# A hand-ordered graph network kernel: spreading a few groups' target columns on TensorE, and a new order for the first turn, the last groups and the value products

## Chip, cores and metric

The kernel runs on one NeuronCore of one Trainium2 chip. The metric is the device time in microseconds of one execution. The core has TensorE (matmuls; its weight loads are shown apart), VectorE, ScalarE, GpSimd (called POOL in the profile) and SyncE, whose queue (SP) issues the transfers.

## What is computed

The input x is 128 graphs of 128 nodes with 256 features, in float32, and adj an integer adjacency matrix of 128 x 128 for each graph (values 0 and 1). Two layers follow each other, each with an attention over the graph, a feed-forward part of 256 to 1024 to 256 and two layer norms:

```python
# layer 0
q, k = x @ Wq + bq, x @ Wk + bk                      # 8 heads of 32
attn = softmax(q k^T / sqrt(32))
out  = sum over r of (attn * (adj == r)) @ (x @ Wv[r] + bv[r])
x = norm(x + out @ Wo + bo)
x = norm(x + gelu(x @ W1 + b1) @ W2 + b2)
# layer 1: two graph attentions, one after the other
def gat(h, W, a):
    Wh = h @ W
    e = leaky_relu(Wh @ a[:F] + transpose(Wh @ a[F:]), 0.2)   # source + target
    return softmax(where(adj > 0, e, -9e15), axis=1) @ Wh
h = norm(x + gat(gat(x, V1, a1), V2, a2))
out = norm(h + relu(h @ U1 + c1) @ U2 + c2)
```

The target term is one number for each node, and it has to be added along the other axis of the 128 x 128 edge matrix: a column of 128 partitions must become a row that all 128 partitions hold. This is the "spread" that the change touches.

## The kernel before, in words

**Groups.** The 128 graphs are cut into 32 groups of G = 4 (512 tokens; NG = 32). All work of a group is on tiles of 128 partitions. A second, general pass stands behind a flag that a few checks compute at the end (`checks`, L755; `pflag`, L858); with these inputs it doesn't run.

**Steps.** Each stage of a group is a Python generator that issues its instructions up to a `yield`; one such piece is a step below. `in_order(...)` (L530) takes generators with counts, and functions, and calls them in turn. So the order in which each engine receives its instructions is written out by hand; nothing is rearranged later. The engines run at their own pace and wait for each other by semaphores.

The generators and their steps:

- `projections` (L552), 8 steps: four products for q and k (tile pq, L560; biased by ScalarE, L564), then four value products, one for each graph (tile pv, L570; VectorE adds the bias into v, L574). They are called pv0 to pv3 in this document.
- `attention` (L647): scores (tile ps, L588; exp on ScalarE into e, L594), mask (pm, L602), sums (denominator pden, L615; pav, L624; two reciprocals, L639 and L641), for two pairs of graphs, then the output product (pwo, L662), which `added` adds to x with the statistics of the norm (L310 to L317).
- `norm` (L358), 4 steps. The first is `root`: VectorE adds epsilon to the variance (rs, L324), GpSimd raises it to the power -1/2 (L325). The second is `normed`: for norms 0 to 2, VectorE forms the shift sh (L333) and ScalarE applies scale and shift to the four blocks of x (L338); for norm 3, VectorE does it (L343). The third and fourth are `scaled`: VectorE multiplies x by a row and adds a row (L356).
- `turned(S, i)` (L370): eight transposes of x into two PSUM tiles (pt, L290), scaled out to yT by ScalarE (L293), and, where a feed-forward follows, four combinations of quarters of yT on VectorE (yS, L378 to L381). i says after which norm. "Turn (31,2)" below is `turned` of group 31 after norm 2.
- `ffn` (L383), 22 steps: both products in a seven-product form (Strassen-Winograd), whose forms are B11, T3, T2, B21, T1, T4 and B22. Steps 1 to 6 and 8 are B11, T3, T2, B21, T1, T4, B22 for the first half of the hidden units; step 7 is B11 for the second half, steps 9 to 14 the rest of it (L400). Steps 15 to 21 are the seven products of the second matrix (L409), 22 the statistics of pair 0. Some products accumulate on a PSUM bank that ScalarE has copied from another (`seeded`, L438, L472, L487); two others are copied out as p7 and p16 (tile p, L445 and L449), and T1 of each half may only start on the bank once p16 is copied. After each, ScalarE applies the activation (L424) and VectorE adds (L455, L459, L468 to L470; L492 to L513 in the second product).
- `layer1` (L705), 12 steps: the product with the combined weights (pw, L713; two steps), the spread of the targets (step 3), the edge weights in three steps (gs: ScalarE adds source and target, L686; leaky ReLU on VectorE, L690, and exp on ScalarE, L691; mask and normalising on VectorE, L695 to L702), the product py (L726, step 7), the second spread (step 8), three steps of edge weights again, and the product pg (L738) with `added` for norm 2 (step 12).

`spread` (L669) turns the four columns of a group into one 4 x 128 line by one transpose (L672), copies the line to SBUF (L674), sends it to HBM and back as a broadcast to 128 partitions (two transfers on SP's queue, L677 and L678).

**The turns.** The main loop (`for g in range(NG - 1)`, L794) interleaves three groups. Its turn g runs the first feed-forward of group g+1 (f1) and the second of group g (f2), the attention of group g+2 (pr for projections, at for attention), the layer norms n0 to n3, layer 1 of group g in the first half and the first part of layer 1 of group g+1 in the second half. `g == 0` has an order of its own. The turn with g = 30 has no group g+2 (`more` is false). Behind the loop the last group's norm, layer 1 and second feed-forward are written out, then the checks and the last norm, which is done in pairs of graphs so that a pair can be stored while the other is still computed.

The explicit `exp` and `gelu` entries (L526) load ScalarE's function table ahead of its use.

PSUM: four banks rotate under the tag "s" (pq, pv, ps, pden, pt, pw, py, pg, pr); four single banks are for the feed-forward products (three) and pav.

Of the kernel before, what the change touches and what calls it, by code (L numbers as in the profile page):

```python
# [106 lines left out]
def fast_pass(ctx, tc, a, out):  # L107
# [47 lines left out]
    def entered(g):  # L155

        xt = load_xT(g)
        ad, xr = load_rest(g)
        return dict(xt=xt, ad=ad, x=xr, g=g)
# [3 lines left out]
    first = dict(g=0, xt=load_xT(0))  # L163
# [134 lines left out]
    def pair(p):  # L298
        return slice(2 * p, 2 * p + 2)
# [27 lines left out]
    def normed(S, i, bs=slice(0, G)):  # L327
# [3 lines left out]
        if i < 3:  # L331
            sh = small.tile([P, G], F32, tag="sh", name=f"sh_{i}_{S['g']}")
            nc.vector.scalar_tensor_tensor(  # L333
                sh, mv[:, :, 0], -1.0, rs, op0=ALU.mult, op1=ALU.mult
            )
        for b in range(bs.start, bs.stop):
            if i < 3:
# [331 lines left out]
    def spread(columns, n):  # L669

        pr = ps_s.tile([P, T], F32, tag="s", name="pr_" + n)
        nc.tensor.transpose(pr[:G, :P], columns, k.ident)  # L672
# [32 lines left out]
    def layer1(S):  # L705
# [14 lines left out]
        target = spread(wh[:, :, D + 3], n + "_0")  # L720
# [10 lines left out]
        target = spread(yh[:, :, D + 1], n + "_1")  # L731
# [42 lines left out]
    with tc.manual_schedule(engines={ET.PE, ET.Activation, ET.DVE, ET.SP, ET.Pool}):  # L774
# [19 lines left out]
        for g in range(NG - 1):  # L794
# [8 lines left out]
            ready = (lambda: prepared(S2)) if more else (lambda: None)  # L803
            if g == 0:
                in_order((f1, 2), n1_, pr, (f1, 2), lambda: turned(S, 1), (n1_, 2))
                l1 = layer1(S)
                in_order(
                    f1, l1, f1, l1, f1, l1, (f1, 2), pr, (f1, 4), pr, f1, (l1, 3), f1, pr, f1, l1, f1,
                    l1, pr, f1, pr, f1, (l1, 3), f1, pr, f1, l1, n2, (at, 2), f1, n2, f1, n1, pr,
                    lambda: turned(S, 2), (at, 3),  # L810
                )
            else:
                n3 = norm(st[g - 1], 3)
                in_order(
                    pr, lambda: turned(S1, 0), pr, f1, f2_, n3, f1, n0_, (f1, 4), n0_, (f1, 2), n3, l1, f1, f1, l1, n3,
                    (f1, 3), pr, n3, lambda: store(st[g - 1]), f1, f1, exp, l1, l1, pr, f1, l1, f1,
                    f1, l1, n2, f1, at, n2, at, f1, pr, lambda: turned(S, 2), pr, (at, 3), f1, f1, pr, n1,
                )
            if not more:
# [3 lines left out]
                f2, pr, f2, n1, (n2, 2), f2, at, (f2, 2), lambda: turned(S1, 1), (f2, 2), at, (n1, 2),  # L823
                (f2, 2), l1, at, ready, (f2, 4), l1, f2, at, f2, l1, (f2, 2), at, at, f2, at, n0, l1, f2,
                n0, l1, gelu, f2, l1, f2,
            )
            n0_, f2_ = n0, f2
        in_order((f2, 2), n1, (f2, 2), lambda: turned(S1, 1), (n2, 2))
        l1 = layer1(S1)
        in_order(  # L830
            f2, (l1, 2), f2, l1, (n1, 2), (f2, 8), (l1, 3), f2, l1, f2, l1, (f2, 4), (l1, 3), f2, l1,
        )
        n2, n3 = norm(S1, 2), norm(S, 3)
        in_order(n2, f2, n2, (f2, 2), lambda: turned(S1, 2))
# [4 lines left out]
        for p in (1, 0):  # L839
# [5 lines left out]
            if p == 1:  # L845
                in_order((f2, 2))
# [345 lines left out]
```

## Time and profile before

| | |
|---|---|
| device time, 3 runs | 2836.33 us median (2835.97 to 2838.88) |
| span of the profiled execution | 2837.9 us |
| mean granted TensorE clock | 0.991 |
| TensorE busy, 0 to 71 us / 71 to 142 / 142 to 213 | 59.3 / 66.3 / 67.4 of 71 us |
| TensorE busy, 300 to 1200 us | 898.6 of 900 us |
| TensorE busy, 2694 to 2765 / 2765 to 2838 us | 60.2 of 71 / 46.5 of 73 us |
| granted clock there | 0.91 / 0.83 |
| VectorE, ScalarE busy, whole span | 2176.8, 1568.5 us |
| transfers of the spread back from HBM | 64 of 256 KB, 4.2 us to landing |

A page of this profile shows each engine's busy time, its share of the span and its instructions; then the span in 40 slices, in tenths. A line of the waits says which engine's instruction waited for which other, for how long in total, how often, and the longest. In a timeline, a line is a start in us, a duration, engine, source line, operation, what is written and read, and a count of equal instructions merged; brackets hold the idle time before and what ended it. The duration of a merged matmul line reaches to the modelled end of the last one, so the distance between two starts says more of the pace than the duration does. A float32 matmul shows as two instructions: `x4` is two matmuls.

### The profile page before, as it was taken

The page shows a single profiled execution, that of the slowest core. Times are in us where ns is not written, and L with a number is a line of the kernel's source. Part 1 is how long each engine was busy: PE and PEld are TensorE (multiplying, and loading weights), DVE is VectorE, ACT ScalarE, POOL GpSimd, SP SyncE. Part 2 cuts the span into 40 slices and gives each one's busy share as a digit, 9 for nine tenths or more (in the row PEclk, how much of TensorE's full clock was granted, in tenths as well). Part 3 has the DMA queues.
Part 4 walks back from the last instruction along what each step waited for, and adds up shares of the span by engine and source line. Part 5 has one row for each costly group of instructions (what it writes and reads, how often), then busy time and mean ns, then how long its engine had stood idle before and what let it go on. Part 6 is the DMA issues. An engine that isn't in the chain of part 4 may idle for free.

```text
span 2837.9 us, 51798 instructions
## 1 busy us (share of the span) xinstructions
PE 2776.8 (98%) x20816; PEld 2233.8 (79%) x20816; DVE 2176.8 (77%) x5068; ACT 1568.5 (55%) x3395; POOL 162.2 (6%) x153
## 2 busy tenths in 40 slices
PE   8999999999999999999999999999999999999986
PEld 4778788887888887888887887887887887888875
DVE  6677887877787877777877777778778778878765
ACT  3545555556555556555556565556556555555552
POOL 3000000000000000000000000000000000000000
PEclk9999999999999999999999999999999999999998
DMA  6010110010111010111010111000110001110000
GB/s 173 5 27 15 32 35 34 24 34 12 34 35 34 23 35 12 35 34 34 23 35 12 35 34 34 24 26 21 34 35 27 31 15 32 35 34 23 16 16 20
DMA packets 70645, 87.27 MB, mean 31 GB/s; under 512 B 8192, under 2 KB 48512, under 8 KB 70400
## 3 DMA queue, kind: packets, MB, share of 16 engines
q1 hardware_dynamic: 69568, 83.52, 9.5%
q8 instruction: 164, 2.69, 0.4%
q14 instruction: 81, 0.66, 0.1%
q10 hardware_dynamic: 832, 0.40, 0.0%
HBM read 66.99 MB, written 16.91 MB: 30 GB/s over the span
## 4 chain that ended last, share of the span: by engine, by line
PE 86%; ACT 7%; DVE 2%; issue 0%; POOL 0%; POOLq 0%; DVEq 0%; ACTq 0%
PE ph L400 14%; PE po L409 14%; PE seeded L409 12%; PE seeded L400 11%; PE pq L560 7%; PE pv L570 6%; PE pw L713 4%; PE pav L624 4%; ACT x L338 4%; PE pwo L662 4%; PE pt L290 3%; PE pden L615 2%; PE py L726 2%; PE pg L738 2%; ACT e L594 1%; PE ps L588 1%
## 5 line engine op out<-in xcount | busy, mean ns | idle before, releaser
L338 ACT ACTIVATE x<-x,sh,rs 128x256 f32<-128x256 f32 x384 | 199.4, 597 | 180.5 <-DVE sh L333 180.5
L325 POOL TENSOR_TENSOR rs<-rs,mhalf 128x4 f32<-128x4 f32 x129 | 138.8, 1076 | 2635.0 <-DVE rs L324 2225.5
L594 ACT ACTIVATE e<-ps 128x512 f32<-128x512 f32 x256 | 131.8, 601 | 209.1 <-PE ps L588 209.1
L570 PE MATMUL pv<-wv,xT 128*128 128x512 f32 x512 | 242.3, 597 | 0.3 <-ACT e L594 0.3
L400 PE MATMUL seeded<-yS,w_L_gnn_w_ff 128*128 128x256 f32 x768 | 207.3, 392 | 5.0 <-ACT seeded L472 1.3
L400 PE MATMUL seeded<-yS,w_L_gnn_W 128*128 128x256 f32 x768 | 204.0, 388 | 2.4 <-ACT seeded L472 1.3
L455 DVE TENSOR_TENSOR hT<-seeded,p 128x512 f32<-128x512 f32 x128 | 88.5, 692 | 148.3 <-PE seeded L400 148.3
L400 PE MATMUL ph<-yT,w_L_gnn_w_ff 128*128 128x256 f32 x768 | 199.0, 388 | 0.0
L310 DVE BATCH_NORM_STATS2 st<-x 128x6 f32<-128x256 f32 x512 | 192.5, 418 | 7.7
L400 PE MATMUL ph<-yT,w_L_gnn_W 128*128 128x256 f32 x768 | 194.4, 382 | 2.4 <-ACT yT L293 2.4
L409 PE MATMUL po<-w_L_gnn_W,hT 128*128 128x128 f32 x1536 | 190.1, 277 | 0.0
L409 PE MATMUL po<-w_L_gnn_w_ff,hT 128*128 128x128 f32 x1536 | 187.0, 275 | 0.0
L409 PEld LDWEIGHTS po<-w_L_gnn_w_ff,hT 128*128 128x128 f32 x1536 | 184.0, 192 | 3.2
L409 PEld LDWEIGHTS po<-w_L_gnn_W,hT 128*128 128x128 f32 x1536 | 181.7, 192 | 5.7 <-issue 0.5
L400 PEld LDWEIGHTS seeded<-yS,w_L_gnn_W 128*128 128x128 f32 x768 | 138.4, 190 | 52.7 <-issue 15.6
L400 PEld LDWEIGHTS seeded<-yS,w_L_gnn_w_ff 128*128 128x128 f32 x768 | 137.8, 190 | 48.9 <-ACT p L449 24.6
L400 PEld LDWEIGHTS ph<-yT,w_L_gnn_W 128*128 128x128 f32 x768 | 144.2, 191 | 38.0 <-ACT yT L293 10.2
L400 PEld LDWEIGHTS ph<-yT,w_L_gnn_w_ff 128*128 128x128 f32 x768 | 139.2, 191 | 38.3 <-issue 13.9
L602 DVE TENSOR_TENSOR pm<-e,adj 128x512 f32<-128x512 f32 x256 | 161.7, 693 | 4.1 <-ACT e L594 4.1
L686 ACT ACTIVATE gs<-spread,wh 128x128 f32<-128x128 f32 x128 | 40.9, 390 | 187.1 <-DMA spread<-hbm 187.1
L424 ACT ACTIVATE hT<-hT,c_L_gnn_b 128x256 f32<-128x256 f32 x256 | 109.4, 497 | 61.4 <-DVE hT L455 60.3
L570 PEld LDWEIGHTS pv<-wv,xT 128*128 128x128 f32 x512 | 90.7, 192 | 66.1 <-issue 63.6
(155 smaller groups left out, 6116.4 us busy)
## 6 DMA issues: line engine op xcount, KB each, us to landing
xT<-in_xT_dram SPq DMA_DIRECT2D x32, 512.0 KB, 7.1
x<-in_x_dram SPq DMA_DIRECT2D x32, 512.0 KB, 8.3
spread<-hbm SPq DMA_DIRECT2D x64, 256.0 KB, 4.2
out_dram<-x SPq DMA_DIRECT2D x31, 512.0 KB, 2.9
adj<-in_adjT_dram SPq DMA_DIRECT2D x32, 256.0 KB, 6.0
w_L_gnn_W<-in_L_gnn_W_dram SPq DMA_DIRECT2D x8, 256.0 KB, 7.3
w_L_gnn_w_ff<-in_L_gnn_w_ff_dram SPq DMA_DIRECT2D x8, 256.0 KB, 5.1
hbm<-line SPq DMA_DIRECT2D x64, 2.0 KB
```

Source lines behind the costliest of these rows:

```text
L310: nc.vector.bn_stats(st[:, b % 2, :], S["x"][:, b, :])
L325: nc.gpsimd.tensor_tensor(rs[:, bs], rs[:, bs], k.mhalf[:, bs], op=ALU.pow)
L338: nc.scalar.activation(x[:, b, :], x[:, b, :], AF.Identity, bias=sh[:, b : b + 1], scale=rs[:, b : b + 1],)
L400: nc.tensor.matmul(bank[:, s * TH : (s + 1) * TH], wa[:, form, 0, f * P : (f + 1) * P], m, start=start and s == 0, stop=True, skip_group_c ...
L409: nc.tensor.matmul(bank[:, s * P : (s + 1) * P], m[:, f, s * P : (s + 1) * P], wb_[:, form, f, :], start=start and s + f == 0, stop=True, ...
L560: nc.tensor.matmul(pq, w[:, c, m * P : (m + 1) * P], xt[:, c, :], start=(c == 0), stop=(c == NCH - 1),)
L570: nc.tensor.matmul(pv, xt[:, c, b * P : (b + 1) * P], wv[:, c].rearrange("p r d -> p (r d)"), start=(c == 0), stop=(c == NCH - 1),)
L594: nc.scalar.activation(e[:, s], pss[s], AF.Exp, scale=SCALE)
L602: nc.vector.tensor_mul(pm[:, s], S["e", p][:, s], S["ad"][:, pair(p), None, :].to_broadcast([P, 2, NCH, P]),)
L624: nc.tensor.matmul(pav[s * DH : (s + 1) * DH, u, c, :], v[:, d0 : d0 + DH], m[:, s, u, c, :], start=(r == 0), stop=(r == 1),)
L662: nc.tensor.matmul(po[:, s * D : (s + 1) * D], oT[:, c, b * P : (b + 1) * P], wo[:, c, :], start=(c == 0), stop=(c == NCH - 1),)
L713: nc.tensor.matmul(pw[:, :NU], yT[:, c, b * P : (b + 1) * P], wu[:, c, :], start=(c == 0), stop=(c == NCH - 1),)
```

## The change

1. Each group carries a number `direct`. With 0 both of its spreads are direct, with 1 only the second, with 2 none. Groups 0 and 31 have 0, group 30 has 1, all others 2. A direct spread is four matmuls, one for each graph: the stationary operand is the column, repeated 128 times by a stride of zero, the moving operand is the identity. The product holds the column as a row on all partitions, in PSUM, and ScalarE reads it from there. The transpose, the copy and both transfers of such a spread fall away.
2. In turns g = 1 to 29, the value product pv1 moves from behind turn (g,2) to ahead of it; in all of these turns the last value product, pv3, moves from between steps 1 and 2 of the second feed-forward to behind the second step of norm 1.
3. Turn g = 0 has a new order: layer 1 starts and ends earlier, exp is loaded explicitly between its two attentions, the scores of group 2 stand between feed-forward steps 19 and 20, and three value products lie around turn (0,2).
4. Group 29's step 21 of the second feed-forward (B22) moves from the end of its turn to behind turn (31,0). In turn g = 30, turn (30,2) moves behind steps 21 and 22 and norm 1's first step.
5. Behind the loop, layer 1 of group 31 is interleaved with the feed-forward of group 30 earlier; norms 1, 2 and 3 are spread out differently, as are the store of group 30 and the checks. Steps 20 to 22 of group 30's feed-forward come after group 31's pg.
6. The last norm of group 31 is interleaved over its two pairs, and, as it is done by pairs, `normed` now takes the form with sh and ScalarE there.

```diff
-        return dict(xt=xt, ad=ad, x=xr, g=g)
+        return dict(xt=xt, ad=ad, x=xr, g=g, direct={NG - 1: 0, NG - 2: 1}.get(g, 2))
...
-    first = dict(g=0, xt=load_xT(0))
+    first = dict(g=0, direct=0, xt=load_xT(0))
...
-        if i < 3:
-            sh = small.tile([P, G], F32, tag="sh", name=f"sh_{i}_{S['g']}")
+        scalar = i < 3 or bs.stop - bs.start < G
+        if scalar:
+            sh = small.tile([P, G], F32, tag="sh", name=f"sh_{i}_{S['g']}_{bs.start}")
             nc.vector.scalar_tensor_tensor(
-                sh, mv[:, :, 0], -1.0, rs, op0=ALU.mult, op1=ALU.mult
+                sh[:, bs], mv[:, bs, 0], -1.0, rs[:, bs], op0=ALU.mult, op1=ALU.mult
             )
         for b in range(bs.start, bs.stop):
-            if i < 3:
+            if scalar:
...
-    def spread(columns, n):
+    def spread(columns, n, direct):
         pr = ps_s.tile([P, T], F32, tag="s", name="pr_" + n)
+        if direct:
+            for b in range(G):
+                nc.tensor.matmul(
+                    pr[:, b * P : (b + 1) * P], columns[:, b : b + 1].to_broadcast([P, P]), k.ident,
+                    start=True, stop=True,
+                )
+            return pr.rearrange("p (b i) -> p b i", b=G)
...
-        target = spread(wh[:, :, D + 3], n + "_0")
+        target = spread(wh[:, :, D + 3], n + "_0", S["direct"] == 0)
...
-        target = spread(yh[:, :, D + 1], n + "_1")
+        target = spread(yh[:, :, D + 1], n + "_1", S["direct"] < 2)
...
+            ahead = lambda: turned(S, 2)
             if g == 0:
-                in_order((f1, 2), n1_, pr, (f1, 2), lambda: turned(S, 1), (n1_, 2))
+                in_order((f1, 2), n1_, pr, (f1, 2), lambda: turned(S, 1), f1, (n1_, 2), f1)
                 l1 = layer1(S)
                 in_order(
-                    f1, l1, f1, l1, f1, l1, (f1, 2), pr, (f1, 4), pr, f1, (l1, 3), f1, pr, f1, l1, f1,
-                    l1, pr, f1, pr, f1, (l1, 3), f1, pr, f1, l1, n2, (at, 2), f1, n2, f1, n1, pr,
-                    lambda: turned(S, 2), (at, 3),
+                    l1, l1, l1, f1, l1, f1, pr, l1, (f1, 2), l1, pr, (f1, 2), l1, f1, pr, l1, (f1, 2), exp, l1, l1, pr, f1, l1, f1,
+                    f1, l1, n2, f1, at, n2, at, f1, pr, pr, lambda: turned(S, 2), (at, 3), f1, f1, pr, n1, pr
                 )
             else:
                 n3 = norm(st[g - 1], 3)
                 in_order(
-                    pr, lambda: turned(S1, 0), pr, f1, f2_, n3, f1, n0_, (f1, 4), n0_, (f1, 2), n3, l1, f1, f1, l1, n3,
+                    pr, lambda: turned(S1, 0), pr, *(() if more else (f2_,)), f1, f2_, n3, f1, n0_, (f1, 4), n0_, (f1, 2), n3, l1, f1, f1, l1, n3,
                     (f1, 3), pr, n3, lambda: store(st[g - 1]), f1, f1, exp, l1, l1, pr, f1, l1, f1,
-                    f1, l1, n2, f1, at, n2, at, f1, pr, lambda: turned(S, 2), pr, (at, 3), f1, f1, pr, n1,
+                    f1, l1, n2, f1, at, n2, at, f1, pr, pr, *((ahead,) if more else ()), (at, 3), f1,
+                    f1, pr, n1, *(() if more else (ahead,)),
                 )
...
             in_order(
-                f2, pr, f2, n1, (n2, 2), f2, at, (f2, 2), lambda: turned(S1, 1), (f2, 2), at, (n1, 2),
+                (f2, 2), n1, pr, (n2, 2), f2, at, (f2, 2), lambda: turned(S1, 1), (f2, 2), at, (n1, 2),
                 (f2, 2), l1, at, ready, (f2, 4), l1, f2, at, f2, l1, (f2, 2), at, at, f2, at, n0, l1, f2,
-                n0, l1, gelu, f2, l1, f2,
+                n0, l1, gelu, f2, l1, *((f2,) if g + 3 < NG else ()),
             )
             n0_, f2_ = n0, f2
-        in_order((f2, 2), n1, (f2, 2), lambda: turned(S1, 1), (n2, 2))
+        in_order(f2, n1, (f2, 2), lambda: turned(S1, 1))
         l1 = layer1(S1)
         in_order(
-            f2, (l1, 2), f2, l1, (n1, 2), (f2, 8), (l1, 3), f2, l1, f2, l1, (f2, 4), (l1, 3), f2, l1,
+            (f2, 2), (l1, 3), f2, l1, (f2, 2), l1, n1, (f2, 2), l1, n1, (f2, 2), l1, f2, l1, n2, f2, l1, l1, n2, (f2, 3), l1, (f2, 2), l1,
         )
         n2, n3 = norm(S1, 2), norm(S, 3)
-        in_order(n2, f2, n2, (f2, 2), lambda: turned(S1, 2))
+        in_order(n2, f2, n2, (f2, 3), lambda: turned(S1, 2))
         f2 = second_ffn(S1)
-        in_order((f2, 14), (n2, 2), (n3, 4), lambda: store(S), (f2, 2))
+        in_order(f2, n3, (f2, 3), n2, n3, (f2, 4), n2, n3, (f2, 4), n3, lambda: store(S), (f2, 2))
         checks()
-        in_order((f2, 4))
+        in_order((f2, 6))
+        root(S1, 3, pair(1))
+        in_order(f2)
+        normed(S1, 3, pair(1))
+        in_order(f2)
+        root(S1, 3, pair(0))
         for p in (1, 0):
-            root(S1, 3, pair(p))
-            normed(S1, 3, pair(p))
+            if p == 0:
+                normed(S1, 3, pair(0))
             for step in range(2):
                 scaled(S1, 3, step, (p,))
             store(S1, pair(p))
-            if p == 1:
-                in_order((f2, 2))
```

## The prediction

> **What bounds the kernel now.** I read the page's busy shares and slices first, to learn which engine to follow.
>
> ```profile
> PE 2776.8 (98%) x20816; PEld 2233.8 (79%) x20816; DVE 2176.8 (77%) x5068; ACT 1568.5 (55%) x3395; POOL 162.2 (6%) x153
> ...
> PE   8999999999999999999999999999999999999986
> ```
>
> TensorE is full except in the first slice and the last two. So only three things can pay: the start, the end, and stalls in the middle too short to lower a tenth. The waits of TensorE, taken alone, say what it waits for (us in total, times, longest):
>
> ```profile
> PE pt L290 <- ACT x L338: 12.4, 20, 4.0
> PE pflag L858 <- DVE good L856: 7.2, 1, 7.2
> ...
> PE py L726 <- DVE gs L702: 5.1, 2, 4.3
> PE seeded L409 <- DVE x L496: 4.8, 1, 4.8
> PE pg L738 <- DVE gs L702: 4.4, 2, 3.1
> ```
>
> Asked by window, all of these fall before 200 us or after 2640 us, and none between. In those waits nothing is queued for TensorE that doesn't hang on a norm or on the edge weights.
>
> For the short stalls I laid out one middle turn (group 14) in TensorE's timeline and compared starts with those of the same instructions undisturbed.
>
> ```profile
> 1273.86 1.30 PE L290 MATMUL pt<-ident,x 128*128 128x128 f32 x8
> 1275.00 1.88 PE L570 MATMUL pv<-wv,xT 128*128 128x512 f32 x4
> ...
> 1288.67 1.13 PE L400 MATMUL ph<-yT,w_L_gnn_w_ff 128*128 128x256 f32 x4
> 1289.89 1.13 PE L400 MATMUL seeded<-yS,w_L_gnn_w_ff 128*128 128x256 f32 x4
> ```
>
> Eight transposes are followed after 0.87 us elsewhere (1205.12 to 1206.00), here after 1.14: 0.27 lost waiting for x from ScalarE. B21 is followed by T1 after 0.89 elsewhere (1243.46 to 1244.35), here after 1.22: 0.33 lost. ScalarE's timeline shows for what:
>
> ```profile
> 1286.81 0.58 ACT L445 COPY p<-ph 128x512 f32<-128x512 f32 x1 [2.01 <-PE ph L400]
> 1287.29 2.08 ACT L338 ACTIVATE x<-x,sh,rs 128x256 f32<-128x256 f32 x4
> 1289.27 0.57 ACT L449 COPY p<-seeded 128x512 f32<-128x512 f32 x1
> ```
>
> T1 needs that last copy, and the copy stands behind four norm activations. These 0.60 us return in each of the 29 turns g = 1 to 29.
>
> **What the Trainium skill says.** "TensorE: Matmul & The Clock Gate", Part 1, puts an idle TensorE at half clock and lets it back after about 3.4 us of activity. The trace agrees on the price: after the 4.25 us wait at 2756 the py products take 3.60 us to the next start instead of 1.74. It differs on the onset: a 1.93 us wait at 2695 is already followed by 3.51 us instead of 1.73. Part 4 of the same page would explain that, since transposes don't count as busy, and eight precede that wait. Its section "Architectural detail" calls VectorE and ScalarE strict FIFO; the 4.8 us wait above agrees: `x L496` stood behind norm work. "ScalarE: Activation LUTs", What ACT_TABLE_LOAD costs, says about 1283 ns; the trace has 1.28 us.
>
> **The loop (29 turns).** The old order is step 20, pv0, turn, pv1, sums; the new one is step 20, pv0, pv1, turn, sums. The transposes start 1.72 us later (one pv), at about 1275.6. Their x is complete at 1272.27 + 2.08 = 1274.35, so the 0.27 goes. Behind them: yT ends at about 1277.6 (two activations, 1.45), VectorE's four yS at 1278.8, and the reciprocal, which now starts at 1278.67, slips by 0.1 to 0.2. VectorE is packed from there to rs L324 at 1284.46, so rs slips by the same.
>
> The second move puts pv3 behind T3 (step 2) and the norm's second step. The copy p7 then ends at about 1285.2. POOL's power ends about 1286.0, and sh, no longer behind the add of pv3 (1285.95 now), follows at once. The four activations run to 1288.2 and the copy for T1 ends at 1288.7; TensorE reaches T1 at 1289.2. The 0.33 goes too. Behind sh on VectorE now stands the add of pv3 (0.66): ready at 1286.4, done by 1287.0, and the scores, which need its PSUM buffer, start at 1287.2. The margins are 0.2 to 0.5 us. Value 0.60 x 29 = **17.4 us**; ends: 0.75 (the T1 weight load prefetched as well) x 29 = 21.8, and a loss if the margins fail, below.
>
> **The direct spread (five of 64).** Removed each: one transpose (0.11 on TensorE), one copy (0.27 on VectorE), two DMAs on SP's queue. Added: four f32 matmuls of 128x128. No row shows them; the nearest is L409, 16 instructions for 8 such matmuls in 1.785 us, so 8 instructions are 0.89. Net +0.78 each, at the bottleneck: 3.9 in all. It can't gain on TensorE itself; if the broadcast weights load slower, at most the 0.19 of a load row replaces 0.112: 8 x 0.08 = 0.6 more each. I take 0.78. What it removes is latency: ScalarE's wait for spread of 5 to 7 us (7.06 at 2771.77). Where the DMA was hidden, as in group 30 (its gs followed the exp table load), it is pure cost.
>
> **First turn (g = 0).** From 104 to 178 us I compared starts with undisturbed ones: 112.08 to 117.92 holds 3.6 of work in 5.8 (2.2 lost); py 1.0; 153.46 to 169.21 holds 8.2 in 15.75 (7.5 lost, of it some 2.8 at the lower clock: pv 3.78 against 1.88); 173.18 to 175.41, 1.3. The new order is that of the loop, which doesn't lose these. It puts layer 1 earlier, with exp among the gelus, so two more table loads of 1.28 on ScalarE; that lies beside 1.72 us q/k products and T3, T2, where ScalarE idles. I keep 3.5 as remaining and the first 1.0 of the 2.2: gain 12.0 - 4.5 - 1.6 for two spreads = 5.9, taken as **6 us** (2 to 9).
>
> **The end (2690 to 2838).** Lost now, and kept by the new order:
>
> 1. Turn (31,0): 4.1 now. B22 of group 29 (1.79) moves behind the transposes. yT is held at 2696.4 by ScalarE's table load either way, so only the slow stretch shortens: 3.0 kept, +1.1.
> 2. Group 30's second edges: the table load still sets it: 1.6 kept, spread added: -0.8.
> 3. Turns (30,2) and (31,1): 6.3 now, since transposes wait for x with B22 unused behind them. B22 goes ahead; x of (30,2) comes at 2730.3 and of (31,1) at about 2735.2, each some 1 us late, yT 0.4: 3.5 kept, +2.9.
> 4. Group 31's first edges: 7.7 now (py 4.25 plus slow matmuls, T2 0.8). gs is read from PSUM four steps earlier. Kept: T2 1.6 (gs ahead of its copy on ScalarE), py 0.6, spread and its wait 1.1: +4.4.
> 5. Second edges: pg 3.25 plus 1.8 slow; kept 2.3 for the spread, which waits for yh, and one T2: +2.8.
> 6. Turn (31,2): 7.8 now. T4 and B22 (3.6) are held back to cover part of the norm's chain; 5.5 kept, +2.3.
> 7. Last feed-forward: VectorE's 4.85 wait and 1.66 slow go, as scaling, n3 and store are spread over steps 3 to 13. VectorE has about 21 us of work for TensorE's 25: 1.5 kept, +5.2.
> 8. After the last matmul (2823.8) 14.1 remain. The normalising of both pairs moves to ScalarE and is interleaved: VectorE's chain from the last add falls from 8.0 to about 6.7: +1.3. The root and store of pair 1 come later, but pair 0 still ends last.
>
> Sum 19.2. I take off 2.2 for clock lost after the short waits that I placed at full speed: **17 us** (8 to 24).
>
> **Sum.** 17.4 + 6 + 17 = 40.4 against this execution's span of 2837.9: 2797.5. The runs have a median of 2836.3, 1.6 below the span, so 2795.9: 2796.
>
> **Rivals.**
> - *The ends only.* The transposes' 0.27 and T1's 0.33 turn into the same wait at the scores or the sums, because VectorE is as packed as before. For it: margins of 0.2 us; against: the reciprocal has 0.59 of idle ahead of it. 2836.3 - 23 = 2813 (2806 to 2820). Chance 0.20.
> - *The loop, and little at the ends.* The end chains run over VectorE, ScalarE and POOL, none of them shorter; filling TensorE earlier leaves a wait later, and the spreads cost 3.9. Head and end give 5: 2836.3 - 22.4 = 2814 (2808 to 2824). Chance 0.09.
> - *Slower: VectorE's queue in the loop.* The later turn pushes yS, reciprocals, rs and POOL's power by the full 1.72 us; sh waits, with the add of pv3 queued behind it, and the scores wait for that buffer. Per turn 1.72 - 0.6 = 1.1 worse than now, 29 x 1.1 = 32 against 23 from the ends: +9, 2845. It decides from 0.6 + 23/29 = 1.4 us of slip; I reckon 0.2. Chance 0.05.
> - *No change* (within 0.2%, 5.7 us): half such a slip, which eats what the ends bring. 2836. Chance 0.04.
> - My forecast, all three parts (2786 to 2806): 0.62.
>
> About 0.2% is what a measurement of this kernel can tell from no change. Faster: 0.62 + 0.20 + 0.09 = 0.91, less 0.01 for the upper edge; same 0.04; slower 0.06. The range for 8 in 10 runs from the low end of the forecast, 2786, to 2818, which leaves out the slower and equal cases and the tops of the two middle ones.
>
> **What would show it.** In a middle turn: transposes followed after 0.87 to 0.9 us, B21 by T1 after 0.89, the period 85.1 instead of 85.72 (1200.02 to 1285.74). In the first turn no wait of ps for `x L317`. At the end: no wait for `x L496`, py's and pg's for gs L702 under 1.5, some 3 us left before pt of group 31. I am wrong if the period stays at 85.7 (first rival), if ps waits for `v L574` (third), or if the end's total of waits stays above 20 us (second).

## The result and the profile after

The changed kernel takes **2789.23 us** (median of 4 runs, 2789.1 to 2789.69). The kernel before, run beside it, takes 2837.61 us (4 runs, 2835.97 to 2839.44). The ratio is 0.983 with a 95% interval of 0.9813 to 0.9847: 48.4 us less, 1.7%. The forecast was 40 us less. One later run of the kernel before, at a granted clock of 0.846, took 3183 us and is left out of every number here.

First the page of the kernel after: busy time of each engine, and TensorE's 40 slices in tenths.

```profile
PE 2749.7 (99%) x20851; PEld 2237.4 (80%) x20851; DVE 2178.0 (78%) x5061; ACT 1577.8 (57%) x3402; POOL 162.4 (6%) x153
...
PE   8999999999999999999999999999999999999997
```

TensorE executes 35 instructions more (five direct spreads with eight for one) and is busy 27 us less. So the 27 us must be clock and short stalls, which the modelled busy time includes: 16.1 of them lie in the 29 turns of the loop, where the granted clock is 1.00 in both, 7.0 at the end and 4.0 before the loop. The two last slices were 8 and 6 and are now 9 and 7. The loop's tenths can't show anything.

To place the gain I cut both executions at two marks that are the same instruction in both: the transpose of the first spread of group 1 (second half of turn 0) and that of group 30 (second half of turn 29). Between them lie 29 equal periods. The view is the one by windows: length, then busy time and instructions of TensorE, its weight loads, VectorE, ScalarE and GpSimd, then the granted clock, the DMA share and GB/s. The end of the kernel before:

```profile
2679.64:2837.90 158.26, 121.03 (x704) 104.22 (x701) 95.28 (x257) 59.66 (x130) 7.75 (x8) 0.88 0.06 18
```

The end of the kernel after:

```profile
2652.52:2787.40 134.88, 114.02 (x725) 99.63 (x722) 92.99 (x252) 60.55 (x134) 8.26 (x8) 0.95 0.04 15
```

The lengths of all three stages from the same view:

| stage | before | after | gain | forecast |
|---|---|---|---|---|
| start and first turn | 193.46 | 186.15 | 7.3 (0.4 of it in the initial loads) | 6 |
| 29 turns | 2486.18, 85.73 each | 2466.37, 85.05 each | 19.8 (0.683 each) | 17.4 |
| end | 158.26 | 134.88 | 23.4 | 17 |
| span | 2837.9 | 2787.4 | 50.5 | 40.4 |

All three parts came true and all three are somewhat larger. At the end, TensorE's idle time (length less busy time) falls from 37.2 to 20.9, by 16.4 us. Its busy time falls by 7.0 although 21 instructions were added: that is clock, 0.95 instead of 0.88. What TensorE still waits for at the end, from the view of the waits in that window (us in total, times, longest):

```profile
PE pflag L871 <- DVE good L869: 4.1, 1, 4.1
PE pt L290 <- ACT x L339: 3.9, 11, 1.8
...
PE pg L747 <- DVE gs L711: 1.2, 1, 1.2
```

With the four left out (2.2, 0.9 and 0.9, for copies and yT of ScalarE, and 0.4 of py for gs) they sum to 13.6 us; the same window before summed to 30.5. The wait behind `x L496` (4.8) is gone, and those of py and pg for gs (L702 then, L711 now) fell from 4.3 and 4.4 to 0.4 and 1.2.

Now the middle turn, in TensorE's timeline (start, duration, and the count of merged instructions). It is the same group's turn as in the prediction, 15.45 us earlier in this execution: its first value product pv0 starts at 1256.69 here and started at 1272.14 before.

```profile
1260.13 1.04 PE L290 MATMUL pt<-ident,x 128*128 128x128 f32 x8
1261.10 1.07 PE L616 MATMUL pden<-e,ones 128*32 128x512 f32 x8
...
1272.95 1.13 PE L401 MATMUL ph<-yT,w_L_gnn_w_ff 128*128 128x256 f32 x4
1273.92 1.03 PE L401 MATMUL seeded<-yS,w_L_gnn_w_ff 128*128 128x256 f32 x4
1274.78 1.04 PE L290 MATMUL pt<-ident,x 128*128 128x128 f32 x8
```

B21 (ph) is followed by T1 (seeded) after 0.97 instead of 1.22, and T1 by the transposes after 0.86; before, T1's own four matmuls took 0.97, since its first weight load started only with T1 itself (1289.89); now that load starts 0.21 ahead of T1. The transposes are followed after 0.97 instead of 1.14, and the value product that stood behind them took 1.82 instead of 1.72. Both signs that the prediction named, 0.87 to 0.9 and 0.89, are missed by 0.07 to 0.1: TensorE waits for no other engine in either place any more, but 0.97 is what these instructions take there.

The sum of the turn is this. The first move brings 0.17 at the transposes and 0.10 at the value product, 0.27. The second brings 0.25 between B21 and T1, 0.11 in T1, and 0.07 in the two products behind T1's transposes (1.73 instead of 1.80). That makes 0.70, by which 27 of the 29 periods are shorter; two are 0.28 longer than the others, and the mean falls by 0.683.

ScalarE's timeline of the same stretch:

```profile
1270.75 2.08 ACT L339 ACTIVATE x<-x,sh,rs 128x256 f32<-128x256 f32 x4 [0.79 <-DVE sh L334]
1272.73 0.56 ACT L450 COPY p<-seeded 128x512 f32<-128x512 f32 x1
```

And VectorE's:

```profile
1270.55 0.16 DVE L334 SCALAR_TENSOR_TENSOR sh<-mv,rs 128x4 f32<-128x4 f32 x1 [1.21 <-POOL rs L325]
1271.09 0.69 DVE L575 TENSOR_TENSOR v<-pv,r_L_gnn_bv 128x512 f32<-128x512 f32 x1 [0.38 <-PE pv L571]
```

The copy that T1 needs ends at 1273.29, 0.6 ahead of T1. With 15.45 added, rs (1269.18) is at 1284.63 (before: 1284.46, so it slipped by 0.17), sh at 1286.00, the copy's end at 1288.74 and T1 at 1289.37; the prediction had worked out a slip of 0.1 to 0.2, then 1286.0, 1288.7 and 1289.2. The bracket of the last line matters for what follows: the add of pv3 waits for its product on TensorE, not for sh.

### The profile page after: what moved, and what is told of

Its sections match the earlier page's. It is cut to its first block, busy times and chain, and to the rows that moved or that the text cites. A ratio compares the mean times of both kernels' runs of the same rounds, so it can differ in the third digit from the quotient of the medians.

```text
span 2787.4 us, 51876 instructions
## 1 busy us (share of the span) xinstructions
PE 2749.7 (99%) x20851; PEld 2237.4 (80%) x20851; DVE 2178.0 (78%) x5061; ACT 1577.8 (57%) x3402; POOL 162.4 (6%) x153
## 4 chain that ended last, share of the span: by engine, by line
PE 94%; DVE 2%; ACT 2%; DMA 1%; issue 1%; SPq 1%; POOL 0%; ACTq 0%; POOLq 0%; DVEq 0%
PE po L410 16%; PE ph L401 16%; PE seeded L401 12%; PE seeded L410 12%; PE pq L561 7%; PE pv L571 7%; PE pw L722 4%; PE pwo L663 4%; PE pav L625 4%; PE pt L290 3%; PE ps L589 2%; PE pden L616 2%; PE py L735 2%; PE pg L747 2%; ACT x L339 1%
## 5 line engine op out<-in xcount | busy, mean ns | idle before, releaser
L339 ACT ACTIVATE x<-x,sh,rs 128x256 f32<-128x256 f32 x388 | 201.6, 597 | 217.3 <-DVE sh L334 217.3
L571 PE MATMUL pv<-wv,xT 128*128 128x512 f32 x512 | 235.5, 593 | 0.0
L695 ACT ACTIVATE gs<-spread,wh 128x128 f32<-128x128 f32 x120 | 38.3, 390 | 186.7 <-DMA spread<-hbm 186.7
```

The lines of the kernel that those rows point to most:

```text
L339: nc.scalar.activation(x[:, b, :], x[:, b, :], AF.Identity, bias=sh[:, b : b + 1], scale=rs[:, b : b + 1],)
L571: nc.tensor.matmul(pv, xt[:, c, b * P : (b + 1) * P], wv[:, c].rearrange("p r d -> p (r d)"), start=(c == 0), stop=(c == NCH - 1),)
```

## The experiments

Every run was compared with the kernel before on the same chip. Periods and ends are cut at the marks above, in one trace each. The kernel after was not run again beside these kernels, so where a difference from its 2789.23 us is only a few us, the length of the stage in the traces is the better measure.

| kernel | us, median | ratio to before (95%) | period | end |
|---|---|---|---|---|
| both value products moved, nothing else | 2818.49 | 0.9933 (0.9917 to 0.995) | 85.03 | 158.1 |
| pv1 alone | 2828.65 | 0.9972 (0.9962 to 0.9983) | 85.47 | 154.5 |
| pv3 alone | 2823.75 | 0.9952 (0.9936 to 0.9969) | 85.30 | 156.2 |
| after, value products moved back | 2810.04 | 0.9904 (0.9887 to 0.992) | 85.75 | 135.1 |
| after, one reciprocal ahead of norm 1 | 2795.88 | 0.9853 (0.9837 to 0.987) | 85.25 | 135.7 |
| after, two reciprocals | 2817.94 | 0.9933 (0.9916 to 0.995) | 86.04 | 135.7 |
| after, no direct spread | 2800.73 | 0.9876 (0.9859 to 0.9892) | 85.05 | 139.5 |
| after, all 64 spreads direct | 2834.18 | 0.9994 (0.9987 to 1.0001) | 86.58 | 135.2 |
| before, new first turn | 2830.06 | 0.9981 (0.9973 to 0.999) | 85.75 | 155.9 |
| after, old last norm | 2791.62 | 0.9838 (0.9821 to 0.9854) | as after | 137.8 |
| after, matmuls before the last turn | 2786.99 | 0.9825 (0.9808 to 0.9841) | as after | 133.5 |
| after, three edits | 2785.37 | 0.9818 (0.9802 to 0.9834) | as after | 131.1 |

**The loop: is it both moves, and do they add up?** The theory is the prediction's 0.27 and 0.33 a turn; the rival is "the ends only", in which the wait returns elsewhere. The first kernel makes both edits in the kernel before, the second and third one each, the fourth takes both out of the kernel after.

```diff
-                    f1, l1, n2, f1, at, n2, at, f1, pr, lambda: turned(S, 2), pr, (at, 3), f1, f1, pr, n1,
+                    f1, l1, n2, f1, at, n2, at, f1, pr, pr, lambda: turned(S, 2), (at, 3), f1, f1, pr, n1,
...
-                f2, pr, f2, n1, (n2, 2), f2, at, (f2, 2), lambda: turned(S1, 1), (f2, 2), at, (n1, 2),
+                (f2, 2), n1, pr, (n2, 2), f2, at, (f2, 2), lambda: turned(S1, 1), (f2, 2), at, (n1, 2),
```

> The kernel before with the two moves of value products alone (pv1 ahead of turn (g,2), pv3 behind T3 and norm 1's second step). Theory: each turn loses the 0.27 and the 0.33 to 0.42 that the two trace places show, the period falls from 85.72 to about 85.03, and the time falls by 29 x 0.69 = 20 us (18 to 21). Rival (the end orders and the loop depend on each other, part of the 20 us came from the first turn's new order carried into the loop): under 12 us.

> The kernel before with pv1 alone moved ahead of turn (g,2). Theory: the transposes no longer wait for x, 0.27 a turn, 7.8 us; the wait of T1 for its copy stays at 0.33. Rival (VectorE's packed queue passes the later turn on to rs and sh, and T1 waits longer): the 0.27 comes back as a longer wait of T1, 0 to 3 us in all.

> The kernel before with pv3 alone moved. Theory: T1 finds its copy ready and its weights loaded ahead, 0.33 to 0.44 a turn, 10 to 13 us; the transposes of turn (g,2) keep their 0.27. With the run of pv1 alone the two add up to the run of both. Rival (the two moves only work together): under 5 us.

> The changed kernel with both value products put back in the loop. Theory: period 85.72 again, 29 x 0.69 = 20 us slower than the changed kernel, so 28 us (27 to 30) faster than before, of which some 7 lie in the first turn and the rest behind the loop. Rival (the loop's gain needs the new ends): within 8 us of the changed kernel.

Both moves alone give 18.0 us (2836.51 to 2818.49; 20.4 by the 29 periods; the difference is put down to the end, whose time varies, see below), and their period, 85.03, is that of the kernel after. Taken out of the kernel after they cost 20.8. So the loop's part stands by itself, whatever is done to the ends. Each move takes away its own wait and leaves the other. TensorE's timeline of pv1 alone, where T1's delay is still there (1284.73 to 1285.95, 1.22):

```profile
1284.73 1.13 PE L400 MATMUL ph<-yT,w_L_gnn_w_ff 128*128 128x256 f32 x4
1285.95 1.13 PE L400 MATMUL seeded<-yS,w_L_gnn_w_ff 128*128 128x256 f32 x4
```

And that of pv3 alone, where the transposes still hold up what follows (1267.12 to 1268.26, 1.14), while T1 follows B21 after 0.97 (1281.93 to 1282.90):

```profile
1267.12 1.30 PE L290 MATMUL pt<-ident,x 128*128 128x128 f32 x8
1268.26 1.88 PE L570 MATMUL pv<-wv,xT 128*128 128x512 f32 x4
```

The periods fall by 0.264 and 0.433, and by 0.702 for both: they add up, and pv3 is worth 0.1 more than the 0.33, being the 0.25, 0.11 and 0.07 named above. In whole times the two give 7.9 and 12.8 us.

**How near was the third rival?** It said that VectorE's queue would be pushed so far that the scores wait for the add of pv3. To find where this begins, that queue is pushed by one or two VectorE reciprocals of a spare 128x96 tile that nothing reads, in front of norm 1 in each of the turns 1 to 29. One takes 0.74 us. From the add of the value product before it, rs comes after 0.58 us in the kernel after, after 1.24 with one reciprocal and after 2.02 with two: it slips by 0.66 and 1.44.

```diff
+        spare = k.tile([P, 96], "spare")
+        nc.vector.memset(spare, 1.0)
...
+            idle = lambda: nc.vector.reciprocal(spare, spare)
...
-                    f1, pr, n1, *(() if more else (ahead,)),
+                    f1, pr, *((idle,) * 2 if more else ()), n1, *(() if more else (ahead,)),
```

> The changed kernel with one extra VectorE reciprocal of 128x96, of no use, ahead of norm 1's root in each of the 29 turns g = 1 to 29. By the trace's 1.66 us for 256 columns it takes some 0.65 us. It moves rs, POOL's power, sh and the add of pv3. Theory (the margin decides; the trace has 0.44 us ahead of the add of pv3 and 0.6 ahead of T1's copy): 0.1 to 0.2 lost a turn, 3 to 6 us. Rival (VectorE's queue is the bound already): the full 0.65 a turn, 19 us. Rival (VectorE has slack beyond a turn's margins): nothing.

> The same with two such reciprocals, some 1.3 us a turn. Theory: the margin is used up by the first, so 0.7 to 0.8 a turn is lost, 20 to 23 us, which gives back the whole gain of the loop: about 2811. Rival (queue is the bound): 38 us, slower than the gain of the loop and most of the ends. Rival (slack): nothing.

One costs 6.7 us, a little above what was expected; two cost 28.7, between the theory (20 to 23) and its rival (38). With two, the rival's wait stands in TensorE's list, 31 times, so about once in a turn:

```profile
PE ps L589 <- DVE v L575: 12.7, 31, 0.4
```

The timeline of that kernel, VectorE's and TensorE's lines of one turn:

```profile
1283.41 0.16 DVE L334 SCALAR_TENSOR_TENSOR sh<-mv,rs 128x4 f32<-128x4 f32 x1 [1.21 <-POOL rs L325]
1283.49 0.68 DVE L575 TENSOR_TENSOR v<-pv,r_L_gnn_bv 128x512 f32<-128x512 f32 x1
...
1284.23 1.15 PE L589 MATMUL ps<-qT,kT 32*128 32x128 f32 x26 [0.41 <-DVE v L575]
```

The add now starts 0.08 after sh, where in the kernel after it starts 0.54 after it, held by its product. So sh may slip by 0.54 - 0.08 = 0.46 us free of charge, and beyond that TensorE pays in full: one reciprocal should cost 0.66 - 0.46 = 0.20 a turn, two 1.44 - 0.46 = 0.98. Measured by the period are 0.205 and 0.99. The idle time in the list, 0.41 a turn, is less than half of it; but from their first start to B21 the scores take 1.99 us with two (1283.32 to 1285.31) against 1.10 in the kernel after, and that is 0.89 of the 0.99. The rival's mechanism is real; what it needs is a slip. The change's own slip was 0.17, inside the margin.

**What are the direct spreads worth, and why only five?** One kernel gives every group the number 2 (none direct), another 0 (all 64 direct).

```diff
-        return dict(xt=xt, ad=ad, x=xr, g=g, direct={NG - 1: 0, NG - 2: 1}.get(g, 2))
+        return dict(xt=xt, ad=ad, x=xr, g=g, direct=2)
...
-    first = dict(g=0, direct=0, xt=load_xT(0))
+    first = dict(g=0, direct=2, xt=load_xT(0))
```

> The changed kernel with all 64 spreads over HBM, its orders kept. The new orders leave 1 to 3 steps between a spread and the addition that reads it. Theory (in groups 0 and 31 the direct spread buys the latency that these orders assume): ScalarE waits 5 to 7 us for each of four spreads, and everything behind it on its queue; each costs TensorE 2 to 6 us with the lower clock, less 0.78 saved: 10 to 20 us slower than the changed kernel. In group 30 the transfer is hidden and 0.78 is saved. Rival (the orders alone do it, the spread is secondary): 4 us faster than the changed kernel, from 5 x 0.78.

> The changed kernel with all 64 spreads on TensorE, 59 more. Theory: in the loop the transfers are hidden and TensorE is the bound, so each costs its 0.78 us: 46 us slower than the changed kernel, about 2835, period 86.6. Rival (the removed copy and the earlier edge weights open room elsewhere): under 25 us.

Without the five, the time rises by 11.5 us, as expected (10 to 20). The traces have 10.5 of it: 5.4 in the first turn, 4.6 at the end, 0.4 in the initial loads. So in the first turn the new order without its direct spreads would keep only some 1.4 of the 6.9 us; direct spreads in the old orders were not run. TensorE's waits at the end of that kernel show the route. ScalarE stands at gs for the transfer, and the copies that TensorE needs stand behind gs:

```profile
PE seeded L401 <- ACT seeded L473: 4.6, 2, 3.9
...
PE seeded L410 <- ACT seeded L488: 3.3, 1, 3.3
```

With all of them direct, 45 us are lost, nearly all that the change brings: the period grows by 1.53, two spreads of 0.77. In a turn of the loop the spread's latency is hidden, though the list of ScalarE's waits in the kernel after has 186.7 us for the transfers, all of which go away here. ScalarE waits for sh instead, 417.4 us against 217.3, so that idle time was not on the path. TensorE's timeline of one such spread, in the kernel with all direct:

```profile
133.84 1.05 PE L676 MATMUL pr<-ident,yh 128*128 128x128 f32 x8
134.73 1.03 PE L401 MATMUL seeded<-yS,w_L_gnn_W 128*128 128x256 f32 x4
```

It takes 0.89 to the next start, so 0.77 more than a transpose of 0.11. The stationary operand repeated by a stride of zero costs nothing extra here.

**The first turn alone.** The kernel before gets the new order of turn g = 0 and the two direct spreads of group 0, as in the change's diff, and nothing else.

> The kernel before with the new order of turn g = 0 and direct spreads for group 0 alone. Theory: the first turn's own waits go, 7 us (6 to 8); nothing changes behind it. Rival (what is won at the start is waited for in the next turn, since the norms' chain has not become shorter): under 3 us.

It is 5.3 us faster by the medians (2835.36 to 2830.06), a little below what was expected. From the first transposes of turn (1,0) to the mark, its trace has 82.46 us, exactly that of the kernel after, against 89.32 before: 6.9 us. The difference between 5.3 and 6.9 is put down to the end, whose code is unchanged but whose time varies between executions, below; that isn't shown for the runs of the medians.

**The last norm.** The old order of the last norm, with VectorE doing the normalising, is put back into the kernel after. The theory was that VectorE's chain is 1.3 us longer so; the rival, that the flag of the checks comes later as well and ends last.

```diff
-        scalar = i < 3 or bs.stop - bs.start < G
+        scalar = i < 3
...
         checks()
         in_order((f2, 6))
-        root(S1, 3, pair(1))
-        in_order(f2)
-        normed(S1, 3, pair(1))
-        in_order(f2)
-        root(S1, 3, pair(0))
         for p in (1, 0):
-            if p == 0:
-                normed(S1, 3, pair(0))
+            root(S1, 3, pair(p))
+            normed(S1, 3, pair(p))
...
+            if p == 1:
+                in_order((f2, 2))
```

> The changed kernel with the last norm of group 31 as before: on VectorE, one pair after the other. Theory of the prediction: VectorE's chain behind the last matmul is 1.3 us longer, and nothing else moves: +1.3 us. Rival (the flag: its reduction follows the last norm on VectorE, and the branch on it ends later than the store; before, pflag ran 0.1 us after the last add began, in the changed kernel 1.8 us before): 3 us (2.5 to 3.5), with pflag again at the last add.

The end is 2.9 us longer (2.4 by the medians), more than the chain accounts for. In the kernel after, VectorE's timeline has the flag ahead of the last multiplications:

```profile
2780.28 0.15 DVE L869 TENSOR_TENSOR good<-good 128x1 f32<-128x1 f32 x1
...
2782.24 0.69 DVE L357 TENSOR_TENSOR x<-x,r_L_gnn_b_ln 128x512 f32<-128x512 f32 x1
```

The span ends at 2787.4, 4.5 us after this last add: the store. With the old norm, the flag comes behind that add:

```profile
2782.94 0.69 DVE L357 TENSOR_TENSOR x<-x,r_L_gnn_b_ln 128x512 f32<-128x512 f32 x1
2783.55 0.14 DVE L870 TENSOR_SCALAR bad<-pflag 1x1 int32<-1x1 f32 x1
```

That span ends at 2789.9, 6.2 after the flag (2783.69), and the kernel before also ends 6.1 after its flag. In the six traces with the old last norm these are 6.0 to 6.3 us, whatever else was changed; in the eight with the new one the span ends 4.3 to 4.7 after the last add. The trace shows what happens between. Every engine loads the flag and branches on it, and TensorE's branch is the long one. In the kernel before (PEldq and PEq are TensorE's queue, SPq that of SyncE; the figures of the first line are ns, then the start in us):

```profile
L1158 PEldq COMPARE_BRANCH  x1: 4452/4452/4452, 2832.4 to 2832.4; - x1
...
SPq L1188 <- PEq L1158: 2.5, 1, 2.5
```

The branch takes 4.45 us, ends at 2836.9, and SyncE has waited for it for 2.5 us; the other engines' branches take 0.05 to 0.08. The last store, issued at 2831.8, had landed after 2.2 us. With the old norm in the kernel after it is the same (4.45 and 2.6). In the kernel after, TensorE's branch ends at 2785.8, and SyncE doesn't wait for it; it waits 2.1 us in its own queue, that of the store.

The store alone would have ended the kernel with the old norm at 2783.63 + 4.5 = 2788.1. So the flag, not the store, ended last before; putting it earlier was worth 1.8, and the shorter chain the rest, 1.2. The flag's instructions stand behind the last norm in the code, in both kernels; the trace has them between its steps, so for them the order is not the written one.

**The clock at the last turn.** The longest wait left at the end precedes turn (31,2), and the two products behind it run slowly (2748.18 to 2751.54, 3.36 us instead of 1.8). In the timeline of the kernel after:

```profile
2745.51 0.33 PE L290 MATMUL pt<-ident,x 128*128 128x128 f32 x1 [1.81 <-ACT x L339]
...
2748.18 2.07 PE L401 MATMUL ph<-yT,w_L_gnn_w_ff 128*128 128x256 f32 x4 [0.43 <-ACT yT L293]
2750.05 1.66 PE L401 MATMUL ph<-yS,w_L_gnn_w_ff 128*128 128x256 f32 x4
```

The theory is that the transposes don't keep the clock up, so that the stretch without matmuls reaches from the end of B22 (it starts at 2741.74 and takes 1.79) to 2748.18 and counts as 4.6 us. The experiment fills the wait with eight matmuls of the identity whose product nothing reads; they can't bring x any sooner.

```diff
-        in_order(n2, f2, n2, (f2, 3), lambda: turned(S1, 2))
+        in_order(n2, f2, n2, (f2, 3))
+        warm = mm_tile("warm")
+        for i in range(8):
+            nc.tensor.matmul(
+                warm[:, (i % G) * P : (i % G + 1) * P], k.ident, k.ident, start=True, stop=True
+            )
+        turned(S1, 2)
```

> The changed kernel with eight more 128x128 float32 matmuls of the identity with itself, read by nobody, between B22 of group 30 and turn (31,2). They lie in a wait for x of 1.8 us. Theory (the slow matmuls behind turn (31,2) are the clock, and transposes don't count as work): B11 and T3 behind it take 1.73 us to the next start instead of 3.36, 1.6 us faster. Rival (transposes count, or the matmuls are slow since their operands come late): no change, or up to 1.8 us slower if they delay the transposes.

The same two products, in that kernel's timeline:

```profile
2742.67 1.95 PE L847 MATMUL warm<-ident 128*128 128x128 f32 x16
...
2747.32 1.13 PE L401 MATMUL ph<-yT,w_L_gnn_w_ff 128*128 128x256 f32 x4 [0.43 <-ACT yT L293]
2748.29 1.03 PE L401 MATMUL ph<-yS,w_L_gnn_w_ff 128*128 128x256 f32 x4
```

They take 1.84 us (T2 starts at 2749.16), 1.5 less, and the transposes come no sooner relative to B22. The granted clock during the two products is 0.53 in the kernel after and 1.00 here, and both wait 0.43 for yT, so late operands are not the cause. The run is 2.2 us faster than the kernel after; in the traces 1.5 of it is the end, the rest the initial loads. So work that is thrown away pays here. That the transposes behind the wait don't count fits, but was not varied by itself: if they counted, the longest stretch without work in the kernel after would be the 2.0 us ahead of them (2743.53 to 2745.51).

**A version that combines this.** Real work can stand where the identity stood. Three edits: the second spread of group 30, which the prediction called pure cost, goes back to the transfer; the exp table of turns 1 to 30 is loaded one step earlier; and one more step of the feed-forward (step 19, T1) is kept for the place between pg and turn (31,2).

```diff
-        return dict(xt=xt, ad=ad, x=xr, g=g, direct={NG - 1: 0, NG - 2: 1}.get(g, 2))
+        return dict(xt=xt, ad=ad, x=xr, g=g, direct={NG - 1: 0}.get(g, 2))
...
-                    (f1, 3), pr, n3, lambda: store(st[g - 1]), f1, f1, exp, l1, l1, pr, f1, l1, f1,
+                    (f1, 3), pr, n3, lambda: store(st[g - 1]), f1, exp, f1, l1, l1, pr, f1, l1, f1,
...
-            (f2, 2), (l1, 3), f2, l1, (f2, 2), l1, n1, (f2, 2), l1, n1, (f2, 2), l1, f2, l1, n2, f2, l1, l1, n2, (f2, 3), l1, (f2, 2), l1,
+            (f2, 2), (l1, 3), f2, l1, (f2, 2), l1, n1, (f2, 2), l1, n1, (f2, 2), l1, f2, l1, n2, f2, l1, l1, n2, (f2, 3), l1, f2, l1,
...
-        in_order(n2, f2, n2, (f2, 3), lambda: turned(S1, 2))
+        in_order(n2, f2, n2, (f2, 4), lambda: turned(S1, 2))
```

> The changed kernel with three edits for waits that its trace still shows: group 30's second spread over HBM again (0.78 of TensorE saved, since its addition waits for the table load either way); exp's table loaded ahead of feed-forward step 15 instead of behind it (the 1.16 us wait of pg in turn 30); step 19 (T1) of group 30 held back behind group 31's pg, so that 1.8 us more of work covers the norm's chain and pg comes 1.8 us earlier (3.8 us of waits and 1.6 of slow clock before the last feed-forward). Theory: 5 us faster than the changed kernel, 2784 (2783 to 2787). Rival (in turn 30 the DMA is late once the table load is early, and VectorE's adds of T1 stand ahead of sh): within 1 us of it.

It takes 2785.37 us (2784.32 to 2785.78), 3.9 below the kernel after, and its end is 3.8 shorter (expected were 5). Of the 3.8, 1.2 come by group 30's second edges, that is from the first two edits: 0.8 for the spread, 0.5 for pg's wait, which falls from 1.16 to 0.68. The other 2.6 come behind. TensorE's timeline shows what the third edit trades:

```profile
2735.11 1.99 PE L747 MATMUL pg<-yh,gs 128*128 128x256 f32 x8 [0.79 <-DVE gs L711]
...
2742.78 0.58 PE L290 MATMUL pt<-ident,x 128*128 128x128 f32 x3
...
2744.72 1.13 PE L401 MATMUL ph<-yT,w_L_gnn_w_ff 128*128 128x256 f32 x4 [0.43 <-ACT yT L293]
```

A wait of 0.79 appears before pg, which T1 had covered, and the wait of 1.81 before the transposes is gone; so is the slow stretch behind it. The three edits were not run one by one.

## Why the prediction was right, point by point

The third column is the gain by starts of the same instructions in the two traces. Only the line between end 5 and end 6 is the end of pg, since the prediction counted pg's own slow pace in end 5 (3.55 us before, 1.89 after).

| step of the prediction | forecast | measured |
|---|---|---|
| the loop, 29 turns | 17.4 | 19.8 |
| first turn | 6 | 6.9 |
| end 1, turn (31,0) | +1.1 | +0.6 |
| end 2, group 30's second edges | -0.8 | -0.7 |
| end 3, turns (30,2) and (31,1) | +2.9 | +3.3 |
| end 4 and 5, group 31's edges | +7.2 | +8.4 |
| end 6, turn (31,2) | +2.3 | +2.5 |
| end 7, last feed-forward | +5.2 | +6.3 |
| end 8, after the last matmul | +1.3 | +3.0 |
| taken off the end for clock | -2.2 | one stretch of 1.5, already in end 6 |
| direct spread, each | +0.78 | +0.77 |

*What bounds the kernel.* Right: the three parts named as the only ones that can pay hold the whole gain, and inside the loop all but 0.07 us a turn lies at the two stalls that were named.

*The loop.* Right in mechanism, as the moves alone and taken out show, and in each date of the chain, within 0.3 us. The term that was mis-sized is 0.60: it is 0.70. The 0.27 is exact. The 0.33 compared B21 with another place, where it takes 0.89; here it takes 0.97 even undisturbed, so the wait was 0.25. T1's own 0.11, its weight load, was left for the upper end (0.75), and the 0.07 behind it was not foreseen.

*Direct spreads.* Right to 0.01 us, from the bound by the nearest row. That group 30's is pure cost fits the version without it: gs has no wait for the transfer there, and TensorE has 0.77 less to do. It wasn't tried alone. The other four are what lets the ends move: without the five, 11.5 of the 48 us are gone.

*First turn.* Right, 0.9 short. The waits of TensorE between 100 us and the mark fell from 6.7 to 3.4 us in total, and ps for `x L317` is gone. The slow stretch that 2.8 us had been counted for is gone too: the granted clock, 0.88 and 0.78 in the two stretches of 10 us from 150 us before, is 1.00 throughout.

*The end.* Every item holds within 1.7 us. Two terms were wrong. Item 8 follows the store and leaves the flag out; the flag ended last, by 1.8 us, and the new order puts it earlier, while the chain that the item does count was worth 1.2, forecast 1.3. And nothing further was lost for clock: of the waits that remain only the one before turn (31,2) drew a slow stretch, of 1.5 us, and end 6 came out as forecast with it. The 2.2 taken off, the 1.7 of item 8, 1.2 of items 4 and 5, 1.1 of item 7 and small differences make the 6.4 us by which the end was better; that nearly all of them have the same sign was not foreseen.

*The sum.* A step that looked harmless was wrong, and it hid a part of the miss. The 40.4 us were reckoned against the profiled execution of before, and this was a long one: 2840.0 us of device time, 3.7 above the median of 2836.3. The device time is 1.7 to 2.3 us above the span of its own execution in every run here (2789.2 and 2787.4, say), so the median doesn't belong to this span. The 2797.5 us of span that the prediction leaves would be some 2799.4 of device time, not 2796. The gain was underrated by 10 us in the traces (50.5 against 40.4), and yet the time was missed by 6.8 only; that is luck. It is also why 50.5 us in the traces are 48.4 in the medians.

*The rivals.* "The ends only" is what remains if the value products are moved back: 2810, forecast 2813. It is refuted for the change as it is, as the period fell. The second falls too: the ends brought 30.7 us in the traces and 26.5 by the medians of the kernel with the value products moved back, not 5. The third was refuted as a forecast and confirmed as a mechanism. It had its deciding slip too low, though: with 0.46 free, 0.68 gained in the loop and 30.7 / 29 = 1.06 from the ends, slower would begin at a slip of about 2.2 us, not 1.4. That is an estimate from these figures; the largest slip that was run is 1.44.

## What to carry to other kernels

When TensorE is 98% busy, compare the distance between starts of the same instructions in a good and in a bad place of one steady turn: two stalls of 0.3 us, invisible in tenths and in the list of waits, were 20 us here. Fill a wait by moving independent work ahead of it in the same queue, and check the queues that the moved wait pushes: the free slip can be read as the idle time that a later instruction there spends on another engine (0.46 us here). Trade TensorE time for latency only where nothing is left to hide the latency: the same spread on TensorE gains at both ends and loses 0.77 us each in the loop. And look at what the program's last instant waits for: here it was a branch, and the store had long landed.

## What was not expected of the hardware

*A stretch without matmuls of about 3.2 us may or may not halve the clock.* In the kernel before, the eight transposes and the wait of turn (31,0) make such a stretch, from 2693.93 to 2697.13, and the two products behind it are slow: the next starts at 2700.64, after 3.51 us, as the prediction noted:

```profile
2697.13 2.06 PE L400 MATMUL ph<-yT,w_L_gnn_W 128*128 128x256 f32 x4 [1.93 <-ACT yT L293]
...
2700.64 1.03 PE L400 MATMUL seeded<-yS,w_L_gnn_W 128*128 128x256 f32 x4
```

In the kernel with only the first turn changed, the same code has the same wait, after a stretch of the same 3.2 us (from 2686.31), and takes 1.83 us to the next start:

```profile
2689.51 1.13 PE L400 MATMUL ph<-yT,w_L_gnn_W 128*128 128x256 f32 x4 [1.93 <-ACT yT L293]
...
2691.34 1.09 PE L400 MATMUL seeded<-yS,w_L_gnn_W 128*128 128x256 f32 x4
```

The granted clock during the two products is 0.51 in the first case and 1.00 in the second. Five traces have this old end: in two the products are slow (3.51 and 3.40 us), in three they are not (1.83). The Trainium skill, "TensorE: Matmul & The Clock Gate", Part 1, calls the window by which the clock is set free-running, so that the same stretch can fall differently in two executions; and by Part 4 transposes don't count as busy in the same way as other matmuls. Both fit. But the window that Part 1 gives is about 3.4 us, a little more than this stretch, and the measurement decides: 3.2 us were enough in two of five. The phase itself no trace shows.

The unchanged end took between 154.5 and 158.3 us in the traces of before and of four kernels that share it, and the runs of before spread over 3.5 us, those of after over 0.6.

*The end of a program may hang on a flag.* From the flag's last VectorE instruction to the end of the span 6.0 to 6.3 us passed in the six traces where it ended last, 4.3 to 4.6 of them in TensorE's branch, against 4.3 to 4.7 from the last add where the store ended last. In the kernel after the two nearly tie: 2780.86 + 6.15 = 2787.0 and 2787.4.
